# Writing the first gather table from the raw node features instead of the normed ones

## The chip, the core and the metric

The kernel runs on one core of a Trainium2 chip. The core has five engines that run their own instruction streams and wait for each other through counting semaphores: PE (the tensor engine, whose weight loads the profile lists as PEld), DVE (vector), ACT (scalar), POOL (GpSimd) and SP (sync, which only issues transfers here). ACT can issue transfers too, and POOL issues the indirect ones, the gathers. The metric is the device time of one execution in microseconds (us), as the median of several runs.

## The reference, cut to what matters

A graph of 6250 nodes with 256 features and 106250 edges (each drawn edge both ways, and one loop per node, sorted by target) goes through two blocks of graph convolution, linear attention and a mixture of experts. Only the first convolution's beginning matters here:

```python
xn = _layernorm(x, axis=-1)
# L0_gnn: two gcn_conv of xn, each with loops added again
deg  = segment_sum(ones, dst)                 # loops included
dinv = where(deg > 0, rsqrt(deg), 0.0)
h = x @ W
msg = h[src] * (dinv[src] * dinv[dst])[:, None]
out = segment_sum(msg, dst) + b
x + relu(out)
# L0_mix: linear attention over the same xn
```

The kernel gathers rows of `dinv * xn` instead of rows of `h`, sums them by target, multiplies by W afterwards and scales by `dinv` of the target. So before the first gather can start there must be a table in device memory, `t1`, with a row `dinv[n] * xn[n]` for every node n. The normed features `xn` themselves are needed in on-chip memory as well: for the residual and for the attention.

## The kernel before

**Tiles.** Nodes lie in 49 tiles of 128 rows (`NT = 49`, `P = 128`); the tile `xa` (128 x 49 x 256 f32) holds all of them on the chip and is updated in place through the whole kernel. Edges lie in 831 chunks of 128.

**Preparation (lines 332 to 461).** SP loads `dst` and then `x` group by group into `xa`; ACT's queue loads `src` in three pieces (lines 341, 343, 344). DVE casts the indices, PE transposes them, DVE builds one-hots and PE counts the degrees with them (lines 405 to 425), so that `deg` (128 x 49) is there. Beside this, `ln_stats` (line 221) makes mean and variance of each tile on DVE with two instructions, in groups of seven tiles: `rstd` (line 226) takes the square root on ACT and the reciprocal on DVE, line 456 makes `shift = -mean * rs` on DVE, and line 459 norms each tile in place on ACT: `xa = rs * xa + shift`. Then `first_table` (line 314) takes the root of the degrees on ACT, its reciprocal `dinv` on DVE, and writes for every group of four tiles `t1s = dinv * xa`, the even tiles of a group on DVE (line 326) and the odd ones on ACT (line 324), into one of three buffers. SP stores each buffer to `t1` (line 327). Last it makes `rdeg`, which is used much later.

**The branch.** `gflag` says whether the edges are spread so unevenly that a general path is needed. It is worked out from the indices (lines 427 to 449), loaded into a register of every engine (line 463), and every engine branches on it by itself (line 466). With these inputs the general path, which makes the degrees and the table again, is not taken. A second branch on the same register (line 496) is in `general_sums`. At such a branch the framework brings the semaphores of both sides to the same counts: on the skipped side, each engine first waits until its own count (SP: the counts of its transfers) has reached what was issued ahead of the branch, and then adds what the other side would have added. Instructions behind the branch wait for these counts.

**Behind the branch (line 653 on).** SP loads W1 (line 657) and other weights. `neighbour_sums` (line 536) goes through the 831 chunks: POOL gathers the rows of a chunk from `t1` (line 552, four chunks to a buffer, four buffers), DVE makes the one-hots (line 556), PE sums with them (line 575). Between the chunks a planner (`pace`) puts pieces of the attention: PE transposes the normed `xa` (line 259), DVE and ACT copy the two halves out (lines 265 and 263) and PE multiplies them (line 687).

**Order.** From there on PE, SP and POOL keep the order in which the code is written (`ORDERED`); DVE and ACT are ordered by the framework's scheduler. In the preparation the scheduler orders the compute engines; SP's transfers there stand as written.

Of the kernel before, what the change touches and what calls it, by code (L numbers as in the profile page):

```python
# [31 lines left out]
F32 = mybir.dt.float32  # L32
BF16 = mybir.dt.bfloat16
I32 = mybir.dt.int32
AF = mybir.ActivationFunctionType
ALU = mybir.AluOpType
AX = mybir.AxisListType

P = 128
N = 6250  # L40
C = 256
NT = 49
# [21 lines left out]
def groups(size):  # L64
    return [(t0, min(size, NT - t0)) for t0 in range(0, NT, size)]
# [73 lines left out]
def gps_kernel(ctx: ExitStack, tc: tile.TileContext, i: dict, out: bass.AP):  # L139
    nc = tc.nc  # L140
    x_in = i["x"]

    def pool(stack, name, bufs=1, side="left", **kw):
        return stack.enter_context(tc.tile_pool(name=name, bufs=bufs, side=side, **kw))

    consts = pool(ctx, "consts")
    edges = pool(ctx, "edges")
    nodes = pool(ctx, "nodes")
    small = pool(ctx, "small", bufs=3)
# [13 lines left out]
    def ps_mm(name):  # L163
        return ps_tile(name, "mm")
# [9 lines left out]
    def tiles_of(t, t0, n):  # L174

        return t[t0 * P:(t0 + n) * P, :].rearrange("(t p) c -> p t c", p=P)
# [34 lines left out]
    deg = consts.tile([P, NT], F32, name="deg")  # L211
    dinv = consts.tile([P, NT], F32, name="dinv")
    rdeg = consts.tile([P, NT], F32, name="rdeg")
    mv0 = consts.tile([P, NT, 2], F32, name="mv0")
    rs0 = consts.tile([P, NT], F32, name="rs0")
    mv1 = consts.tile([P, NT, 2], F32, name="mv1")
    rs1 = consts.tile([P, NT], F32, name="rs1")
    mv2 = consts.tile([P, NT, 2], F32, name="mv2")
# [2 lines left out]
    def ln_stats(mv, row):  # L221
        st = small.tile([P, 6], F32, name="st", bufs=4)
        nc.vector.bn_stats(st, row)
        nc.vector.bn_aggr(mv, st)

    def rstd(rs, var, n):
        sd = small.tile([P, n], F32, name="sd")
        nc.scalar.activation(sd, var, AF.Sqrt, bias=eps_t, scale=1.0)
        nc.vector.reciprocal(rs, sd)
# [53 lines left out]
    t1 = (dram.tile([NPAD, C], F32, name="t1f"), None)  # L283
# [12 lines left out]
    xa = nodes.tile([P, NT, C], F32, name="xa")  # L296
# [14 lines left out]

    gflag = consts.tile([1, 1], I32, name="gflag")

    def first_table(tp):

        sd = small.tile([P, NT], F32, name="sdeg")
        nc.scalar.activation(sd, deg, AF.Sqrt, bias=ones[:, 0:1], scale=1.0)
        nc.vector.reciprocal(dinv, sd)
        for t0, n in groups(4):
            ts = tp.tile([P, 4, C], F32, name="t1s", bufs=3)  # L320
            for t in range(n):
                T = t0 + t
                if t % 2:
                    nc.scalar.activation(ts[:, t, :], xa[:, T, :], AF.Copy, scale=dinv[:, T:T + 1])
                else:
                    nc.vector.tensor_scalar(ts[:, t, :], xa[:, T, :], dinv[:, T:T + 1], None, op0=ALU.mult)
            nc.sync.dma_start(tiles_of(t1[0], t0, n), ts[:, :n, :])
        dmx = small.tile([P, NT], F32, name="dmax")
        nc.vector.tensor_scalar(dmx, deg, 1.0, None, op0=ALU.max)
        nc.vector.reciprocal(rdeg, dmx)  # L330

    with ExitStack() as st:
        prep = pool(st, "prep")
# [2 lines left out]
        for name, fill, q in (("dst", -1, nc.sync), ("src", 0, nc.scalar)):  # L336
            t = prep.tile([P, NBLK, P], I32, name=f"{name}_pre")
# [44 lines left out]
        for name, to in (("dst", dsti), ("src", sp)):  # L382
            pf = prep.tile([P, NBLK, P], F32, name=f"{name}_pf")
            nc.vector.tensor_copy(pf, pre[name])
            for b0 in range(0, NBLK, 4):
                n = min(4, NBLK - b0)
# [18 lines left out]
        for c0 in range(0, NCH, P):  # L405
            n = min(P, NCH - c0)
# [6 lines left out]
            for c in range(c0, c0 + n):  # L413
# [19 lines left out]
                                op0=ALU.subtract)  # L433
# [14 lines left out]
        nc.vector.tensor_scalar(gpen, gpen, 1.0e6, None, op0=ALU.mult)  # L448
        nc.vector.tensor_scalar(lof, lof, gpen, None, op0=ALU.subtract)

        for t0, n in groups(7):
            for T in range(t0, t0 + n):
                ln_stats(mv0[:, T, :], xa[:, T, :])
            rstd(rs0[:, t0:t0 + n], mv0[:, t0:t0 + n, 1], n)
            shift = small.tile([P, 7], F32, name="shift")
            nc.vector.scalar_tensor_tensor(shift[:, :n], mv0[:, t0:t0 + n, 0], -1.0, rs0[:, t0:t0 + n],
                                           op0=ALU.mult, op1=ALU.mult)
            for T in range(t0, t0 + n):
                nc.scalar.activation(xa[:, T, :], xa[:, T, :], AF.Identity, bias=shift[:, T - t0:T - t0 + 1],
                                     scale=rs0[:, T:T + 1])  # L460
        first_table(pool(st, "table0"))

    general = nc.values_load(gflag[0:1, 0:1], min_val=0, max_val=1,
                             skip_runtime_bounds_check_because="it is the result of a comparison")

    with tc.If(general):
        with ExitStack() as st:
            gw_ = pool(st, "gdeg")
            nc.vector.memset(deg, 0.0)
            hi = gw_.tile([P, NCHP], I32, name="g_hi")  # L470
            nc.vector.tensor_scalar(hi, dsti, 7, None, op0=ALU.arith_shift_right)
            hif = gw_.tile([P, NCHP], F32, name="g_hif")
            nc.vector.tensor_copy(hif, hi)
            nc.vector.tensor_scalar(hi, dsti, P - 1, None, op0=ALU.bitwise_and)
            low = gw_.tile([P, NCHP], F32, name="g_low")
            nc.vector.tensor_copy(low, hi)
            with tc.For_i(0, NCH, 1) as c:
                hc = gw_.tile([P, 1], F32, name="g_hc")
                nc.vector.tensor_copy(hc, hif[:, ds(c, 1)])
                lc = gw_.tile([P, 1], F32, name="g_lc")  # L480
                nc.vector.tensor_copy(lc, low[:, ds(c, 1)])
                oh = gw_.tile([P, NT], F32, name="g_oh")
                nc.vector.tensor_scalar(oh, iota_f[:, :NT], hc, None, op0=ALU.is_equal)
                ol = gw_.tile([P, P], F32, name="g_ol")
                nc.vector.tensor_scalar(ol, iota_f[:, :P], lc, None, op0=ALU.is_equal)
                gd = ps_mm("g_deg")[:, :NT]
                nc.tensor.matmul(gd, lhsT=ol, rhs=oh, start=True, stop=True)
                nc.vector.tensor_add(deg, deg, gd)
        with ExitStack() as st:
            first_table(pool(st, "table1"))  # L490

# [696 lines left out]
    with tc.If(general), ExitStack() as st:  # L1188
# [8 lines left out]
        for j, half in ((OWN[0], 0), (OWN[1], 1)):  # L1197
# [3 lines left out]
                                    op0=ALU.mult, op1=ALU.subtract)  # L1201
# [419 lines left out]
```

## Time and profile before

| what | us |
|---|---|
| median of 7 runs | 4454.25 (4450.22 to 4473.68) |
| the profiled execution | 4441.32 |
| its span, first to last instruction | 4439.3 |
| degree ready (DVE, line 425) | 51.3 |
| in-place norms on ACT (line 459) | 15.8 to 76.2 |
| table tiles on DVE (line 326) | 67.1 to 93.0 |
| table tiles on ACT (line 324) | 71.8 to 91.8 |
| stores of t1, issued by SP (line 327) | 72.8 to 93.0 |
| first gather from t1 (POOL, line 552) | 99.0 |
| last gather from t1 | 1310.3 |

All times are counted from the start of the span. The profiled execution is one run of its own; it lies below the median of the others. How to read the lines that follow: in a timeline a line has the start, the duration (of all of a run of equal instructions, if there is a count), engine, line of the code, operation, result and operands, count, and in brackets the idle time of the engine just before and what ended it; "issue" means that the profile shows nothing that was waited for, "remote" an event whose source it doesn't know. A name with a small q (SPq, ACTq) is the sequencer of an engine, which issues transfers, waits and branches. In a list for one line or tile, the durations are min/median/max in ns, and then come the starts of the first and the last. In a table by stage, each engine has its busy time and, in brackets, its instructions; PEclk is the granted clock of the tensor engine.

### The profile page before, as it was taken

Reading aid. Unit: us, or ns where it says so; the run is one execution under the profiler, and the core shown is the slowest. Engines: PE = TensorE matmul, PEld = TensorE weight load, DVE = VectorE, ACT = ScalarE, POOL = GpSimd, SP = SyncE. Lnnn points to the kernel's source line nnn. Section 1 sums busy time; section 2 is a strip of 40 time slices with the busy share of each in tenths; the row PEclk is TensorE's granted clock in tenths of the full one; section 3 lists DMA queues with packets and bytes.
Section 4 is the critical chain, followed back from the end, with each engine's and each line's share of the span. In section 5 each row is a group of like instructions: output and inputs, shape, how many; then the busy total and the mean of one; then the engine's idle time right before and its main releaser. Section 6 shows DMA issues by size and latency. Waiting matters only on the chain. (4 is left out here: it accounts for less than half of the span.)

```text
span 4439.3 us, 60578 instructions
## 1 busy us (share of the span) xinstructions
PE 3314.5 (75%) x23423; PEld 2722.3 (61%) x23423; DVE 1411.3 (32%) x5300; ACT 981.8 (22%) x2048; POOL 2552.3 (57%) x2665
## 2 busy tenths in 40 slices
PE   3788766766655567777777788883788888888888
PEld 2577656655643445555555665673677777677676
DVE  6222221222121223222232322643343333343333
ACT  3111000000001112222222233441122222222222
POOL 1666666666656666666666555113566666666562
PEclk9888766666676778888888898997799998999998
DMA  4455333333344445555555655575444444444442
GB/s 154 130 169 166 115 113 115 115 113 115 114 122 140 131 129 175 176 178 170 154 166 176 202 180 175 173 255 149 114 133 134 133 132 126 131 132 131 129 130 67
DMA packets 341389, 639.63 MB, mean 144 GB/s; under 512 B 57498, under 2 KB 230341, under 8 KB 341088
## 3 DMA queue, kind: packets, MB, share of 16 engines
q0 software_dynamic: 151872, 450.67, 34.9%
q1 hardware_dynamic: 188366, 184.56, 13.2%
q8 instruction: 185, 3.03, 0.3%
q14 instruction: 116, 0.95, 0.1%
q10 hardware_dynamic: 850, 0.43, 0.0%
HBM read 559.64 MB, written 75.80 MB: 143 GB/s over the span
## 5 line engine op out<-in xcount | busy, mean ns | idle before, releaser
L552 POOL DMA_INDIRECT parts<-t3b,sp x831 | 813.0, 978 | 500.7 <-issue 202.4
L552 POOL DMA_INDIRECT rows<-t1f,sp x831 | 807.2, 971 | 494.2 <-issue 221.7
L552 POOL DMA_INDIRECT parts<-t2b,sp x831 | 805.9, 970 | 468.4 <-issue 220.5
L575 PEld LDWEIGHTS <-parts 128*128 128x128 bf16 x9972 | 604.1, 107 | 377.3 <-issue 167.8
L575 PE MATMUL sums<-onehot,parts 128*128 128x84 bf16 (+2 forms) x9972 | 697.1, 215 | 129.6 <-issue 63.7
L575 PE MATMUL sums<-onehotf,rows 128*128 128x84 f32 (+1 forms) x3324 | 576.2, 325 | 244.8 <-issue 182.4
L575 PEld LDWEIGHTS sums<-onehotf,rows 128*128 128x128 f32 x3324 | 564.1, 244 | 292.2 <-issue 267.9
L902 PE MATMUL hid<-ft,fw 128*128 128x256 f32 (+1 forms) x1824 | 545.0, 438 | 100.0 <-DVE ft L265 35.1
L902 PEld LDWEIGHTS hid<-ft,fw 128*128 128x128 f32 x1824 | 364.2, 217 | 166.2 <-issue 43.6
L556 DVE TENSOR_TENSOR onehot<-iota_w,lof 128x336 bf16<-128x336 bf16 x416 | 210.4, 506 | 752.6 <-PE sums L575 315.6
L904 ACT ACTIVATE ht<-hid,fb 128x256 f32<-128x256 f32 (+1 forms) x456 | 208.7, 472 | 430.3 <-PE hid L902 217.9
L778 PE MATMUL h<-w,aggt 128*128 128x256 f32 x392 | 151.7, 525 | 185.2 <-issue 84.0
L556 DVE TENSOR_TENSOR onehotf<-iota_wf,lof 128x336 f32<-128x336 f32 x208 | 104.7, 507 | 582.2 <-remote 390.8
L1088 PE MATMUL exp<-wd,ht 128*128 128x256 f32 x1024 | 263.2, 395 | 13.4 <-ACT ht L904 6.7
L778 PEld LDWEIGHTS h<-w,aggt 128*128 128x128 f32 x392 | 89.6, 252 | 206.9 <-issue 90.1
L1088 PEld LDWEIGHTS exp<-wd,ht 128*128 128x128 f32 x1024 | 187.1, 193 | 42.1 <-issue 11.1
L595 ACT COPY aggt<-sums 128x88 f32<-128x88 f32 x96 | 22.4, 233 | 828.0 <-PE sums L575 465.4
L1060 POOL DMA_INDIRECT ys<-y,to x64 | 64.0, 1001 | 216.9 <-DVE y L1093 96.0
L1434 PE MATMUL fc_ps<-ht,fc 128*128 128x256 f32 (+1 forms) x600 | 161.6, 392 | 5.8 <-issue 3.1
L1446 PE MATMUL fc_ps<-fc,ut 128*128 128x256 f32 x588 | 160.7, 398 | 6.2 <-issue 6.0
L1434 PEld LDWEIGHTS fc_ps<-ht,fc 128*128 128x128 f32 x600 | 104.7, 192 | 17.9 <-issue 3.7
L1446 PEld LDWEIGHTS fc_ps<-fc,ut 128*128 128x128 f32 x588 | 104.4, 193 | 17.5 <-issue 8.0
(355 smaller groups left out, 4325.3 us busy)
## 6 DMA issues: line engine op xcount, KB each, us to landing
wd<-in_L_ffn_Wd SPq DMA_DIRECT2D x64, 1024.0 KB
xs<-zero SPq DMA_DIRECT2D x8, 1799.0 KB
rows<-t1f,sp POOLq DMA_INDIRECT x831
parts<-t2b,sp POOLq DMA_INDIRECT x831
parts<-t3b,sp POOLq DMA_INDIRECT x831
t2b<-t2s SPq DMA_DIRECT2D x49, 192.0 KB
t3b<-t3s SPq DMA_DIRECT2D x24, 384.0 KB
fs<-xs SPq DMA_DIRECT2D x64, 128.5 KB
```

The source lines that it names most:

```text
L552: nc.gpsimd.indirect_dma_start(out=gs[:, j, :], out_offset=None, in_=(table if f32 else parts)[:, :], in_offset=bass.IndirectOffsetOnAxis( ...
L556: nc.vector.tensor_tensor(ohs[:, :n, :], (iota_wf if f32 else iota_w)[:, None, :WIN].to_broadcast([P, n, WIN]), lof[:, c:c + n, None].to_b ...
L575: nc.tensor.matmul(ps[b][:, h, n0 - b * P:n1 - b * P], lhsT=g[:, k * C + h * P:k * C + (h + 1) * P], rhs=oh[:, n0 - w0:n1 - w0], start=Fal ...
L595: nc.scalar.copy(dst[:, :, WIN:], sums[:, :, WIN:P])
L778: nc.tensor.matmul(h, lhsT=at[:, k, :], rhs=w[:, k, :], start=(k == 0), stop=(k == 1))
L902: nc.tensor.matmul(h_ps[:, :w], lhsT=fw1[:, k, m * P:(m + 1) * P], rhs=ft[:, k, :w], start=(k == 0), stop=(k == 1))
L904: nc.scalar.activation(ht[:, m, :w], h_ps[:, :w], AF.Gelu, bias=fb1[:, m:m + 1], scale=1.0)
L1060: nc.gpsimd.indirect_dma_start(out=ys[v][:, :], out_offset=bass.IndirectOffsetOnAxis(ap=to, axis=0), in_=y, in_offset=None)
L1088: nc.tensor.matmul(y_ps, lhsT=ht[:, m, q * P:(q + 1) * P], rhs=wd[:, m, :], start=(m == 0), stop=(m == 7))
L1434: nc.tensor.matmul(u_ps[:, :w], lhsT=fc1[:, k, m * P:(m + 1) * P], rhs=ht[:, k, :w], start=(k == 0), stop=(k == 1))
L1446: nc.tensor.matmul(h_ps, lhsT=ut[:, m, t * P:(t + 1) * P], rhs=fc2[:, m, :], start=False, stop=(m == 5))
```

## The change

`first_table` is split. Its first and last part, `dinv` and `rdeg`, become `factors`, called as soon as the degrees and the flag are worked out. The table is then made straight from the raw features: for each group of five tiles, DVE makes the statistics, the reciprocal root and `shift` as before, and also `rs * dinv` and `shift * dinv` (the two halves of the new small tile `by`); ACT writes `t1s = (rs * dinv) * xa + shift * dinv` for all five tiles, and SP stores the group. There are three buffers of five tiles. Only when all ten groups are written in the code do the 49 in-place norms on ACT follow, still ahead of the branch. DVE makes no table tile any more. `shift` is kept for all 49 tiles. The general path calls `factors` and the old `first_table` again.

```diff
+    shift = consts.tile([P, NT], F32, name="shift")
...
-    def first_table(tp):
+    def factors():
 
         sd = small.tile([P, NT], F32, name="sdeg")
         nc.scalar.activation(sd, deg, AF.Sqrt, bias=ones[:, 0:1], scale=1.0)
         nc.vector.reciprocal(dinv, sd)
+        dmx = small.tile([P, NT], F32, name="dmax")
+        nc.vector.tensor_scalar(dmx, deg, 1.0, None, op0=ALU.max)
+        nc.vector.reciprocal(rdeg, dmx)
+
+    def first_table(tp):
+
         for t0, n in groups(4):
...
-        dmx = small.tile([P, NT], F32, name="dmax")
-        nc.vector.tensor_scalar(dmx, deg, 1.0, None, op0=ALU.max)
-        nc.vector.reciprocal(rdeg, dmx)
...
-        for t0, n in groups(7):
+        factors()
+        tp = pool(st, "table0")
+        for t0, n in groups(5):
             for T in range(t0, t0 + n):
                 ln_stats(mv0[:, T, :], xa[:, T, :])
-            rstd(rs0[:, t0:t0 + n], mv0[:, t0:t0 + n, 1], n)
-            shift = small.tile([P, 7], F32, name="shift")
-            nc.vector.scalar_tensor_tensor(shift[:, :n], mv0[:, t0:t0 + n, 0], -1.0, rs0[:, t0:t0 + n],
-                                           op0=ALU.mult, op1=ALU.mult)
-            for T in range(t0, t0 + n):
-                nc.scalar.activation(xa[:, T, :], xa[:, T, :], AF.Identity, bias=shift[:, T - t0:T - t0 + 1],
-                                     scale=rs0[:, T:T + 1])
-        first_table(pool(st, "table0"))
+            g = slice(t0, t0 + n)
+            rstd(rs0[:, g], mv0[:, g, 1], n)
+            nc.vector.scalar_tensor_tensor(shift[:, g], mv0[:, g, 0], -1.0, rs0[:, g], op0=ALU.mult, op1=ALU.mult)
+            by = small.tile([P, 2, 5], F32, name="by", bufs=3)
+            nc.vector.tensor_mul(by[:, 0, :n], rs0[:, g], dinv[:, g])
+            nc.vector.tensor_mul(by[:, 1, :n], shift[:, g], dinv[:, g])
+            ts = tp.tile([P, 5, C], F32, name="t1s", bufs=3)
+            for t in range(n):
+                nc.scalar.activation(ts[:, t, :], xa[:, t0 + t, :], AF.Identity, bias=by[:, 1, t:t + 1],
+                                     scale=by[:, 0, t:t + 1])
+            nc.sync.dma_start(tiles_of(t1[0], t0, n), ts[:, :n, :])
+        for T in range(NT):
+            nc.scalar.activation(xa[:, T, :], xa[:, T, :], AF.Identity, bias=shift[:, T:T + 1],
+                                 scale=rs0[:, T:T + 1])
...
+        factors()
         with ExitStack() as st:
             first_table(pool(st, "table1"))
```

## The prediction

> **What bounds the kernel now.** I read the page first, then a table of stages (busy time by stretch), then the timeline of the first 130 us, then single lines of code, and last the lists of what each engine's instructions wait for in the built programs, which hold no times.
>
> ```profile
> PE 3314.5 (75%) x23423; PEld 2722.3 (61%) x23423; DVE 1411.3 (32%) x5300; ACT 981.8 (22%) x2048; POOL 2552.3 (57%) x2665
> ```
> ```profile
> core 0: us, PE busy (x) PEld busy (x) DVE busy (x) ACT busy (x) POOL busy (x), PEclk, DMA share, GB/s
> 0.00:51.30 51.30, 28.28 (x850) 24.99 (x850) 41.78 (x93) 9.73 (x19) 9.27 (x49) 1.00 0.50 156
> 51.30:92.00 40.70, 0.69 (x3) 0.50 (x2) 23.32 (x110) 29.36 (x65) 0.00 (x0) 1.00 0.39 131
> 92.00:99.00 7.00, 0.00 (x0) 0.00 (x0) 1.79 (x4) 0.00 (x0) 0.01 (x1) 1.00 0.61 201
> 99.00:1320.00 1221.00, 852.39 (x4512) 766.11 (x4512) 267.35 (x639) 117.74 (x356) 807.50 (x834) 0.73 0.43 126
> ```
>
> Over the whole span the tensor engine does most. The change touches only 51.3 to 99 us. There the second row shows ACT busy 29.4 of 40.7 us and DVE 23.3, PE and POOL next to nothing: the whole core waits for table t1 to be written, because the first gather reads it at 98.99. So what counts is one moment, the release of the first gather; everything later hangs on it in a row (POOL starts a gather nearly every 1.25 us from there). The chain of waits on the page is traced back only to 3058 us, so I read this moment from the timeline:
>
> ```profile
> 96.77 0.51 DVE L556 TENSOR_TENSOR onehotf<-iota_wf,lof 128x336 f32<-128x336 f32 x1 [3.79 <-SPq L466]
> 96.91 0.39 SPq L657 DMA_DIRECT2D w<-in_L_gnn_W  x1
> 98.99 1.11 POOL L552 DMA_INDIRECT rows<-t1f,sp  x1 [89.07 <-DVE onehotf L556]
> 107.29 0.59 ACT L263 COPY xnt<-xtr 128x512 f32<-128x512 f32 x1 [15.47 <-issue]
> 126.60 0.69 DVE L265 COPY xnt<-xtr 128x512 f32<-128x512 f32 x1 [11.31 <-remote]
> ```
> ```profile
> L466 SPq EVENT_SEMAPHORE  x8: 17/17/17, 95.1 to 96.5; - x8
> L466 ACTq EVENT_SEMAPHORE  x1: 17/17/17, 92.0 to 92.0; - x1
> ```
>
> L466 is the branch around the general path. Its skipped side waits until all that was issued ahead of the branch is done, then passes. SP's eight waits there end at 96.5, when the last store of t1 (issued 93.0) has landed; DVE starts 0.3 us later, SP's load of W1 at 96.91, POOL 2.1 us behind it. ACT was through at 92.0 and then had nothing to do until 107.29.
>
> **The point the rest turns on.** After the branch, the first one-hot on DVE, the W1 load on SP and the first gather on POOL each wait for ACT's count as well. In the changed program that count is 136: 111 of ACT's own, which includes the last of the 49 in-place norms, and 25 from the skipped side, which waits for 111. The norms stand ahead of the branch in the program text, so "behind that" is still ahead of the join. The stores end earlier, but the join moves from SP (96.5) to ACT.
>
> ```profile
> L459 ACT ACTIVATE xa<-xa,shift,rs x49: 583/586/612, 15.8 to 75.6; 128x256 f32<-128x256 f32 x49
> L324 ACT ACTIVATE t1s<-xa,dinv x24: 491/492/510, 71.8 to 91.3; 128x256 f32<-128x256 f32 x24
> L326 DVE TENSOR_SCALAR t1s<-xa,dinv x25: 345/348/354, 67.1 to 92.6; 128x256 f32<-128x256 f32 x25
> ```
> ```profile
> 64.76 6.99 ACT L459 ACTIVATE xa<-xa,shift,rs 128x256 f32<-128x256 f32 x14 [0.30 <-DVE shift L456]
> ```
>
> **The change part by part.** (1) Removed from DVE: 25 scalings of 0.348. They and ACT's 24 waited 20.7 us for stores that moved 340 GB/s; that goes too. Neither is a saving by itself, it depends on ACT below.
> (2) ACT before: 14 of its norms lay ahead of 51.3, in the shadow of the degree count. In the changed order none does: up to the degree ACT has three square roots and two copies. From there it has 49 table tiles and 49 norms, 98 activations. Pitch: 14 of them in 6.99 us, (6.99 - 0.587)/13 = 0.493. The new table tile (bias and scale per row, another tile as output) is not in the trace; nearest below is L324, scale alone, 6 in 2.48 us, pitch 0.41; nearest above is 0.586, the norm's full duration without overlap. I take 0.493, same operands as L459. 98 x 0.493 = 48.3 us (49 x 0.41 lower by 4; all at 0.586 higher by 9).
> (3) Start of these 98. The degree is done at 51.3 (50.74 + 0.55). Then DVE's order up to the first `by`: 0.28 + 0.16 + 0.40 + 0.12 + 0.43 + 0.12 + 0.16 + 0.46 + 0.12 + 0.24 from the rows of these lines = 2.5, less the overlap of some 0.07 each: first table tile about 53.7. The degree itself may come later: ACT's second and third load of `src` (L343, L344, issued at 1.6 and 5.2) now stand behind its first square root, which needs the statistics of tile 4, about 10.3 by DVE's row at 9.46. They are issued near 11, while the loads of x fill the DMA engines at 340 GB/s until about 25 us. DVE casts `src_pre` at 14.56, ahead of all the one-hots of the degree, so a landing past 14.6 shifts all. Between 0 and 2 us; I take 1.
> (4) Seven square roots stay between the activations: two took 0.48, so 1.5. Behind the third and the seventh of them ACT waits for DVE (reciprocal, shift, two products): waits for DVE's shift were 0.30 to 0.69 before, with one norm as filler now; 0.5 each, 1.0.
> (5) Statistics: 32 of 49 remain for DVE after the degree, pitch 0.39, 12.5 us; ACT reaches them later than DVE in both rounds (18 x 0.39 end near 62.6, ACT asks at 62). Nothing on the path; without that cover at most 1.
> (6) Stores: 10 instead of 13 on SP, 640 KB each per 2.5 us of ACT against 1.9 at 340 GB/s, three buffers. Hidden. The last, 512 KB, is issued near 82 and lands about 87: hidden behind the norms (23 us). SP has nothing behind them except the W1 load, which waits for ACT anyway. The extra `by` products (20 on DVE, 0.12 each) and rdeg lie in (3) and (4).
> (7) Behind the join: the instructions of PE, POOL and SP are the same in the same order, DVE's and ACT's too. What is queued: DVE's one-hots, POOL's gathers, SP's W1, W2 and clears, then PE. All norms are then done, as before.
>
> Sum: 51.3 + 1 + 2.4 + 48.3 + 1.5 + 1.0 = 105.5, and 0.2 for the last one's end and the wait (ACT's register load overlapped its last activations before): ACT passes at 105.7 instead of SP at 96.5 with DVE 0.3 later. DVE's one-hot moves from 96.77 to about 105.8, the first gather from 98.99 to 108: **9 us later**. With the bounds: low 9 - 1 - 4 - 1 = +3, high 9 + 1 + 9 = +19.
>
> On the profiled execution (4441.3; its span 4439.3 and 2 around it) that makes 4450. It lay 13 us under the median of the seven runs, 4454.25, so for the median I add the same 9: **4463 us, 0.2% slower**. About 0.3%, 13.4 us, is what a measurement of this kernel tells from no change, so this counts as no change.
>
> A rule speaks against this change: the Trainium skill, page "ScalarE: Activation LUTs", section "Rules for kernel authors", says that multiplying and adding belong on the vector engine rather than the scalar engine. The rows agree for this shape, 0.348 against 0.586. By the rule, half the table tiles stay on DVE (idle between its statistics), ACT saves 25 x 0.493 = 12.3 us, and the change would gain 3 us; as written it loses 9.
>
> **The rivals.**
> *ACT slower than its pitch* (other side). Place: the 98 activations. Price: 0.586 instead of 0.493, 98 x 0.093 = 9.1 us more, +18, 4472. It decides from a mean of 0.54, where the sum passes 13.4. For it: many of them carry a count of their own, and L324, broken up into pairs by waits, takes 0.91 for two. Against it: runs of 7 and 14 keep the pitch. 0.15.
> *One more stall behind the branch* (other side). Between 115 and 127 us DVE, ACT and POOL all stood, with a releaser that the profile doesn't know (11.31 us in the row above). If the new start brings one more such stall, 4463 + 11 = 4474; it decides from 4.5 us. For it: such gaps recur, 1.7% of the span (75 us) in the traced chain. Against it: same instructions behind the join, and DVE, SP and POOL stand ready at the branch some 20 us earlier. 0.17. The Trainium skill, page "Runtime: NRT & Kernel Launch", section "Instruction fetch mechanics", has it that a taken branch out of the fetched window stalls until code is loaded; the trace has one packet of code between 115 and 120 and one between 120 and 126 and names no cause; by that rule the sum stays, since the same branches are taken.
> *The join does not hold* and the gathers start when the stores have landed, near 87 + 2.4. Then the table is 9.5 us earlier, but ACT is still busy with norms until 105.7 and its first copy, 107.29 before, comes at about 106; PE stands in order behind it. Gain between 1.4 and 9.5: 4450. Against it: the counts in the program. 0.08. Even the whole 9.5 stays under 13.4, so faster is hardly open.
>
> **How the numbers follow.** Forecast 0.58, the rivals 0.15, 0.17 and 0.08, others 0.02. Slower: 0.32. Faster: a quarter of the last rival and the others, 0.04. Same: the rest, 0.64. The likeliest case by itself runs from 4457 (+3) to 4467; towards the slower cases I go to 4475, below to 4452 for scatter of the medians.
>
> **What would show it.** In the profile after: last store of t1 issued near 82 and landed near 87; in-place norms on ACT without a break from about 82 to 105.5; first one-hot near 105.8, released by ACT and not by SP; first gather near 108; DVE idle over 30 us ahead of it; from there the same order, ending 9 us later. Wrong: a first gather before 95 (no join on ACT), a pitch of the new table tiles away from 0.49, the degree later than 54, or an end that moved by more than the first gather did.

## The result, and the profile after

| | before | after |
|---|---|---|
| median (runs) | 4459.38 us (63) | 4470.70 us (26) |
| range | 4440.54 to 4481.04 | 4444.36 to 4488.32 |
| ratio after / before | | 1.0024, 95% interval 1.0012 to 1.0035 |
| span of the profiled execution | 4439.3 us | 4457.9 us |

The ratio is 10.7 us (5.4 to 15.6) of 4459.38: a loss too small to count as slower by the 0.3% that the prediction set, though the interval excludes no change.

First the table of stages of the changed kernel (start and end, then busy time and instructions of each engine, the granted clock, the DMA share and GB/s), cut where the degree is done, where the branch opens and where the first gather starts:

```profile
core 0: us, PE busy (x) PEld busy (x) DVE busy (x) ACT busy (x) POOL busy (x), PEclk, DMA share, GB/s
0.00:52.83 52.83, 28.29 (x850) 25.00 (x850) 41.92 (x96) 3.05 (x6) 9.28 (x49) 1.00 0.45 152
52.83:104.80 51.97, 0.71 (x3) 0.50 (x2) 17.85 (x109) 49.91 (x106) 0.00 (x0) 1.00 0.37 125
104.80:107.13 2.33, 0.00 (x0) 0.00 (x0) 1.44 (x3) 0.00 (x0) 0.00 (x0) 1.00 0.45 117
```

In the second row ACT is busy 49.9 of 52.0 us, DVE 17.9, and everything else has next to nothing to do. In the kernel before, ACT had done part of its work in the shadow of the degree count; of that, 9.73 us ahead of the degree have become 3.05 here. The timeline shows what ACT does, and who starts when it stops (start, length, engine, line, operation, count, and in brackets the idle time before it with what ended it):

```profile
55.15 7.48 ACT L470 ACTIVATE t1s<-xa,by 128x256 f32<-128x256 f32 x15 [1.95 <-DVE by L467]
...
57.74 24.30 SPq L472 DMA_DIRECT2D t1f<-t1s  x10
62.53 0.67 ACT L229 ACTIVATE sd<-mv,eps_t 128x5 f32<-128x5 f32 x3
63.10 0.59 ACT L474 ACTIVATE xa<-xa,shift,rs 128x256 f32<-128x256 f32 x1
...
72.22 9.43 ACT L470 ACTIVATE t1s<-xa,by 128x256 f32<-128x256 f32 x19
...
81.55 23.17 ACT L474 ACTIVATE xa<-xa,shift,rs 128x256 f32<-128x256 f32 x47
104.79 0.38 SPq L672 DMA_DIRECT2D w<-in_L_gnn_W  x1
104.80 0.51 DVE L571 TENSOR_TENSOR onehotf<-iota_wf,lof 128x336 f32<-128x336 f32 x1 [29.76 <-ACTq L480]
...
107.13 1.11 POOL L567 DMA_INDIRECT rows<-t1f,sp  x1 [97.20 <-DMA w<-in_L_gnn_W]
```

The waits at the branch (L480) of the same kernel:

```profile
L480 SPq EVENT_SEMAPHORE  x8: 17/17/17, 83.2 to 85.0; - x8
...
L480 DVEq EVENT_SEMAPHORE  x1: 21/21/21, 75.7 to 75.7; - x1
...
L480 ACTq EVENT_SEMAPHORE  x1: 17/17/17, 104.8 to 104.8; - x1
```

The table is complete at 81.6 and has landed at 85.0, 11.5 us earlier than before (96.5). The one-hot on DVE still stands until 104.80, 29.76 us, and its releaser is ACT's wait at the branch: the 47 norms from 81.55 to 104.72 are all that the core does for 20 us. The first gather starts 8.1 us later than before (107.13 against 98.99). The bracket at the gather names the load of W1, which itself was let go at 104.79 by the branch.

The single profiled spans differ by 18.6 us, more than that. The gathers show where: 8.1 us at the first gather, 6.6 at the last one from the first table, 7.7 and 11.9 at the two ends of the second table, 16.3 and 21.8 at those of the third. They are two executions out of ranges 40 us wide; a second pair, below, differs by 11.1.

### The profile page after: what moved, and what is told of

Its sections match the earlier page's. It is cut to its first block, busy times and chain, and to the rows that moved or that the text cites. A ratio compares the mean times of both kernels' runs of the same rounds, so it can differ in the third digit from the quotient of the medians.

```text
span 4457.9 us, 60590 instructions
## 1 busy us (share of the span) xinstructions
PE 3329.0 (75%) x23423; PEld 2736.8 (61%) x23423; DVE 1407.6 (32%) x5301; ACT 997.1 (22%) x2076; POOL 2554.5 (57%) x2665
## 2 busy tenths in 40 slices
DMA packets 341341, 639.63 MB, mean 143 GB/s; under 512 B 57450, under 2 KB 230293, under 8 KB 341040
## 5 line engine op out<-in xcount | busy, mean ns | idle before, releaser
L590 PE MATMUL sums<-onehotf,rows 128*128 128x84 f32 (+1 forms) x3324 | 593.0, 332 | 275.9 <-issue 210.1
L590 PEld LDWEIGHTS sums<-onehotf,rows 128*128 128x128 f32 x3324 | 582.0, 251 | 319.4 <-issue 295.9
L917 PE MATMUL hid<-ft,fw 128*128 128x256 f32 (+1 forms) x1824 | 534.7, 432 | 90.7 <-DVE ft L266 34.3
L1103 PEld LDWEIGHTS exp<-wd,ht 128*128 128x128 f32 x1024 | 189.2, 196 | 44.3 <-issue 11.7
L1425 PE MATMUL att<-wf,xnt 128*128 128x256 f32 x196 | 74.2, 528 | 64.6 <-DVE xnt L266 41.9
L1449 PEld LDWEIGHTS fc_ps<-ht,fc 128*128 128x128 f32 x600 | 105.4, 194 | 16.9 <-issue 5.2
```

What stands on the lines that cost most here:

```text
L590: nc.tensor.matmul(ps[b][:, h, n0 - b * P:n1 - b * P], lhsT=g[:, k * C + h * P:k * C + (h + 1) * P], rhs=oh[:, n0 - w0:n1 - w0], start=Fal ...
L917: nc.tensor.matmul(h_ps[:, :w], lhsT=fw1[:, k, m * P:(m + 1) * P], rhs=ft[:, k, :w], start=(k == 0), stop=(k == 1))
L1103: nc.tensor.matmul(y_ps, lhsT=ht[:, m, q * P:(q + 1) * P], rhs=wd[:, m, :], start=(m == 0), stop=(m == 7))
L1425: nc.tensor.matmul(ps, lhsT=xnt[:, k, t * P:(t + 1) * P], rhs=wf[:, k, :], start=(k == 0), stop=(k == 1))
L1449: nc.tensor.matmul(u_ps[:, :w], lhsT=fc1[:, k, m * P:(m + 1) * P], rhs=ht[:, k, :w], start=(k == 0), stop=(k == 1))
```

## The experiments

The runs were made on three chips. The kernel before took 3903.44 us on the chip of the first four, 4455.78 on that of the next four and 3914.08 on that of the last four. Ratios are to the kernel before on the same chip. The changed kernel as it stands was run on the second of these chips and for the result above, where the kernel before takes 4456 to 4459 us; on the two faster chips it was not, so a ratio from there shows what a variant gains on the kernel before, and not on the changed one.

### Does the branch wait for ACT?

The kernel before, with work for ACT added ahead of the branch:

```diff
         first_table(pool(st, "table0"))
+        idle = prep.tile([P, C], F32, name="idle")
+        for _ in range(30):
+            nc.scalar.activation(idle, xa[:, NT - 1, :], AF.Copy, scale=dinv[:, 0:1])
```

> The kernel before, with 30 useless ACT scalings of one tile (128x256) added behind the last table tile, ahead of the branch; nothing of the result changes. Theory (the branch waits for whichever engine ends last, and all of that reaches the end): ACT, done at 92.0 in the kernel before, ends at 92.0 + 30 x 0.493 = 106.8; the first one-hot on DVE moves from 96.77 to 106.8, the first gather from 98.99 to 109.0, the time by +10 us (ratio about 1.0022). Rival (the branch waits for the stores alone, and the loss of the changed kernel comes from its later degree or from further down): the first gather stays at 99.0 and the time is the same.

Measured: 1.0003 (0.9991 to 1.0015). ACT passed the branch at 99.5, not at 106.8, since 16 of the 30 had slipped into the gaps between its table tiles; the first gather came at 101.64. The releaser was ACT as the theory has it, but the dose was too small to be seen in the time. With 60:

> The kernel before with 60 instead of 30 useless ACT scalings ahead of the branch. With 30, 16 filled ACT's gaps and only 14 stood behind the last table tile, so the dose was small. Here 44 stand behind it. Theory (what ACT adds ahead of the branch reaches the end in full): ACT ends at 92 + 44 x 0.493 = 114, first one-hot at 114, first gather at 116.3, 17 us later than in the kernel before; time +17 us, ratio 1.0038 on a chip on which before takes 4456, 1.0044 where it takes 3903. Rival (a later stage takes some of it up): first gather at 116, but the ratio under 1.002.

Measured: 1.0051 (1.0037 to 1.0065), 20 us (14 to 25). The waits at the branch and DVE's first one-hot:

```profile
L469 SPq EVENT_SEMAPHORE  x8: 17/17/17, 95.2 to 96.6; - x8
...
L469 ACTq EVENT_SEMAPHORE  x1: 17/17/17, 116.6 to 116.6; - x1
```
```profile
116.60 0.51 DVE L559 TENSOR_TENSOR onehotf<-iota_wf,lof 128x336 f32<-128x336 f32 x1 [23.61 <-ACTq L469]
```

The stores had landed at 96.6, where the kernel before goes on; the branch opened with ACT at 116.6, 20 us later, and the time grew by 20 us. What ACT adds ahead of this branch reaches the end, in full as far as the interval tells. (The 44 last scalings had a pitch of 0.54, not 0.493, hence 116.6 instead of 114. They have the form of L324, whose pitch was 0.41, but all write one and the same tile; whether that is the reason was not tried.)

### The kernel before and the changed kernel on one chip

> The kernel before, unchanged, profiled on the chip that the experiments run on: the four runs so far took some 3900 us where the recorded ones took 4460, so the yardsticks at the branch have to be read on the same chip. Theory (what lies ahead of the branch is no faster here; the difference between the chips arises behind it): first one-hot at 96 to 97, first gather at 98 to 99, as recorded. Rival (everything is faster here by the 12%): degree at 45, first gather at 87.

Measured: 4451.43, one run; first one-hot at 97.28, first gather at 99.51. This chip turned out to be of the recorded kind, so the question of the faster one was answered elsewhere: on the chip of 3903 us the kernel with 30 added scalings had its stores landed at 96.0 and its first gather at 101.64. Ahead of the branch the chips are alike.

> The changed kernel, unchanged, beside the kernel before on this chip. Theory (the branch opens with ACT's last norm, 49 + 49 operations of 0.493 us behind a degree at 52.4): first one-hot at 104.3, first gather at 106.6, 8 us behind the kernel before, and these 8 us reach the end: ratio 1.0020 with this kernel's time (3903). Rival (part of the recorded loss arises further down): the first gather 8 us late, but the ratio 1.003 or more; or the delay is taken up by a stage further down that waits for something else: ratio 1.000.

Measured: 1.0020 (0.9999 to 1.0040). The gathers of the three tables, in the kernel before and then in the changed one (count, duration, first and last start):

```profile
L552 POOL DMA_INDIRECT rows<-t1f,sp x831: 940/946/1943, 99.5 to 1312.0; - x167
L552 POOL DMA_INDIRECT parts<-t2b,sp x831: 940/946/1261, 1328.4 to 2769.1; - x167
L552 POOL DMA_INDIRECT parts<-t3b,sp x831: 940/946/1944, 3070.8 to 4388.9; - x167
```
```profile
L567 POOL DMA_INDIRECT rows<-t1f,sp x831: 943/949/1276, 107.3 to 1320.4; - x167
L567 POOL DMA_INDIRECT parts<-t2b,sp x831: 942/949/1343, 1336.6 to 2781.0; - x167
L567 POOL DMA_INDIRECT parts<-t3b,sp x831: 942/949/1938, 3083.0 to 4401.9; - x167
```

The difference is 7.8 us at the first gather, 8.4 at the end of that stage, 8.2 at the start of the next, 12 to 13 from its end on, and 11.1 at the end. The first 8 us stay. In both pairs a few us more come behind the second table; they are of the size by which single executions differ, and two pairs cannot tell more.

### Taking the norms out of the branch's way

The 49 norms written behind the branch, in one block. The general path, which reads the nodes too, makes its table from the raw rows with product columns instead:

```diff
             nc.sync.dma_start(tiles_of(t1[0], t0, n), ts[:, :n, :])
-        for T in range(NT):
-            nc.scalar.activation(xa[:, T, :], xa[:, T, :], AF.Identity, bias=shift[:, T:T + 1],
-                                 scale=rs0[:, T:T + 1])
...
             first_table(pool(st, "table1"))
+    for T in range(NT):
+        nc.scalar.activation(xa[:, T, :], xa[:, T, :], AF.Identity, bias=shift[:, T:T + 1],
+                             scale=rs0[:, T:T + 1])
```

> The changed kernel with its 49 in-place norms written behind the branch instead of ahead of it (all on ACT; the general path makes its table from the raw rows with the product columns). Theory: ACT is through with the table at 81.6, the stores have landed at 85.0; the branch opens there: first one-hot at 85.3, first gather at 87.6, 19.5 us less than in the changed kernel and 11.4 less than before. ACT's norms then run from 85 to 108.5, and the first ACT copy of the transposed nodes, which would come at 96, waits behind them until 108.5: up to 12.4 us of the 11.4 may be given back there if PE needs that buffer, nothing if it does not. Ratio to before 0.9974 to 1.0002. Rival (the loss of the changed kernel does not come from the norms ahead of the branch): ratio stays 1.002 although the norms are gone from there.

Measured: 0.9970 (0.9959 to 0.9981), 11.7 us less than before. The timeline:

```profile
81.25 24.19 ACT L510 ACTIVATE xa<-xa,shift,rs 128x256 f32<-128x256 f32 x49
...
84.71 0.51 DVE L577 TENSOR_TENSOR onehotf<-iota_wf,lof 128x336 f32<-128x336 f32 x1 [10.18 <-SPq L483]
...
87.28 1.11 POOL L573 DMA_INDIRECT rows<-t1f,sp  x1 [77.36 <-ACT xa L510]
```

The same norms run at the same time as in the changed kernel, but the releaser of the one-hot is SP's wait for the stores again, and the gathers no longer wait for the norms: the first starts 18 us ahead of the last norm's end at 105.4. (The bracket at the gather names one of these norms; in the repeat of this kernel below it names the load of W1.) This is the part of the change that decides: the same table and the same stores, and 11.7 us less than before instead of 10.7 more, though the two were measured on chips of different speed.

The norms then hold ACT until 105.4, and its first copy of the transposed nodes comes behind them. Whether that costs anything was asked with the norms of four tiles placed just ahead of these tiles' transposes:

```diff
         for gi, (t0, n) in enumerate(gs):
+            for T in range(t0, t0 + n):
+                nc.scalar.activation(xa[:, T, :], xa[:, T, :], AF.Identity, bias=shift[:, T:T + 1],
+                                     scale=rs0[:, T:T + 1])
             transposed(xnt[:, :, t0 * P:(t0 + n) * P], lambda t: xa[:, t0 + t, :], n, "xtr", vs)
```

> The changed kernel with the norms of each group of four tiles written just ahead of that group's transposes, behind the branch, instead of all 49 in one block there. Theory (the branch opens with the stores at 84.7 to 85, as with the block; ACT's first copies of the transposed nodes no longer stand behind 24 us of norms): first gather at 87.3, first ACT copy of the transposed nodes at 95 to 97 instead of 105; if that copy was on the path, up to 9 us less than with the block, ratio 0.9948 to 0.997. Rival (the copy is hidden by PE's sums, which wait for gathers): the same time as with the block, ratio 0.997.

Measured: 0.9992 (0.9977 to 1.0006), first gather at 88.16. That is 11.4 us earlier than in the kernel before on the same chip, and a time that fell by 3.6 us (10.2 less to 2.7 more). This is also the one chip of the three that had the changed kernel: with the norms at their use its first gather comes 19.1 us earlier (88.16 against 107.3) and its median is 17.1 us lower (4448.43 of 12 runs against 4465.49 of 9). The two placements were then run side by side.

> The kernel with the 49 norms in one block behind the branch once more, beside the one with the norms at their use, so that both are read on one chip. Theory (ACT's first copy of the transposed nodes, 9 to 10 us late behind the block, is covered by PE's sums): branch and first gather as in the other (85 to 86, 87.3 to 88.2), the same ratio within 0.1%. Rival (the late copy holds PE): this one 3 to 9 us slower than the one with the norms at their use.

> The kernel with the norms at their use once more, beside the block. Its first measurement was 0.9992 with an interval that reaches 1.0006, while the block, on another chip, had 0.9970. Theory: both gain what the branch gains, 11.4 us: ratio 0.9974 where before takes 4456, 0.9971 where it takes 3903. Rival (norms between the copies, 17 of ACT's first 20 operations behind the branch, hold up the copies of the nodes and of the sums): 0.999 again, over 4 us slower than the block.

Measured: block 0.9966 (0.9952 to 0.9980), at their use 0.9972 (0.9962 to 0.9982). ACT's first copy of the transposed nodes, block first, then at their use:

```profile
106.15 0.56 ACT L264 COPY xnt<-xtr 128x512 f32<-128x512 f32 x1
```
```profile
95.92 0.58 ACT L264 COPY xnt<-xtr 128x512 f32<-128x512 f32 x1 [9.35 <-PE xtr L260]
```

The copy is 10.2 us later and the time the same: the last gather of the first table starts at 1157.9 and 1157.1. The medians are 3901.35 and 3905.10, so the give-back that the first expectation allowed for is not seen. That the placement at the use had only 0.9992 on the other chip did not repeat here; whether the gain is smaller on chips of that kind stays open, and the block was not run there.

### Sharing ACT's work with DVE

Every second tile of a group made on DVE:

```diff
+                if t % 2:
+                    nc.vector.tensor_scalar(ts[:, t, :], xa[:, t0 + t, :], by[:, 0, t:t + 1], by[:, 1, t:t + 1],
+                                            op0=ALU.mult, op1=ALU.add)
+                else:
                     nc.scalar.activation(ts[:, t, :], xa[:, t0 + t, :], AF.Identity, bias=by[:, 1, t:t + 1],
                                          scale=by[:, 0, t:t + 1])
```

> The changed kernel with every second table tile made on DVE (multiply and add with the same two columns), the norms left on ACT. Theory: ACT loses 20 of its 49 table tiles (two of each group of five), 20 x 0.493 = 9.9 us, so it ends at 104.7 - 9.9 = 94.9; DVE's 20 tiles at 0.31 to 0.35 us (6 to 7 us) fit in, since DVE was through at 75.7. First one-hot at 95, first gather at 97.2: 10 us less than in the changed kernel and 1.8 us less than before; ratio to before 0.9996. Rival (ACT's pace is set by DVE's statistics and by columns, not by its own work): ACT ends at 104 as before and the time stays 1.002.

Measured: 1.0003 (0.9992 to 1.0013), first gather at 96.71. The waits at the branch:

```profile
L484 SPq EVENT_SEMAPHORE  x8: 17/17/17, 80.2 to 82.3; - x8
...
L484 DVEq EVENT_SEMAPHORE  x1: 21/21/21, 77.2 to 77.2; - x1
L484 ACTq EVENT_SEMAPHORE  x1: 17/17/17, 94.3 to 94.3; - x1
```

ACT ends 10.5 us earlier than in the changed kernel and is still the last by 12 us. With that the loss is no longer seen, and no gain either; a gain of the 2 us by which the first gather is earlier than the 98.99 before could not be told.

With the in-place norms alternately on DVE and ACT as well (the same `if` around them):

> As the one with the divided table, and every second in-place norm on DVE as well. Theory: ACT ends 24 x 0.493 = 11.8 us earlier again, at 83.1; DVE, through at 75.7 in the changed kernel, takes 44 more operations of 0.31 to 0.35 us and ends at 89 to 91; the branch opens with DVE then, at 89 to 91, the first gather at 91 to 93.5: 6 to 8 us less than before, ratio 0.9982 to 0.9987. Rival (the stores set the branch once the norms are shared): it opens when the stores have landed, 85 or a little later, gather at 87.5, ratio 0.9974. Second rival (what the branch gains is lost again further down): first gather early, ratio 1.000 or more.

Measured: 0.9980 (0.9971 to 0.9989), 7.8 us less than before, first gather at 86.63. The three engines now reach the branch almost together:

```profile
L488 SPq EVENT_SEMAPHORE  x8: 17/17/17, 80.4 to 82.3; - x8
...
L488 ACTq EVENT_SEMAPHORE  x1: 17/17/17, 82.7 to 82.7; - x1
L488 DVEq EVENT_SEMAPHORE  x1: 21/21/21, 84.2 to 84.2; - x1
```

DVE came last, as expected, but at 84.2 and not at 89 to 91: its 19 last norms took 6.22 us, and the tiles before them went in part where DVE had waited for ACT in the changed kernel, 3.9 us there and none here. The gather started 0.65 us earlier than with the norms behind the branch on the same chip. The median is 4.6 us longer, but the two intervals overlap, so no difference is shown.

Table divided and norms at their use:

> The kernel with the norms at their use and every second table tile on DVE. Theory (with the norms gone the branch opens when the stores have landed, and these are limited by the transfer: ten stores of some 650 KB took 27.3 us both where the last one was issued at 82 and where it was issued at 78): the branch opens at 84 to 85, first gather at 86.2 to 87, 1 us before the kernels with the whole table on ACT; ratio within 0.0005 of theirs. Rival (stores wait for table tiles): the last tile is done 4 to 9 us earlier and the first gather comes at 79 to 84.

Measured: 0.9969 (0.9959 to 0.9979), first gather at 86.18. SP's wait for the stores ends at 83.5 instead of 84.8, with the issue of the last store ended at 80.2 instead of 81.8. So the stores end 3.0 to 3.4 us behind the issue of the last one and still follow the last table tile, as the rival has it and not the theory; but that tile is done only 1.6 us earlier, not 4 to 9, and 1.3 us is all that this brings. In the time it cannot be told.

### Why was the degree late?

> The changed kernel with the three loads of src issued on SP, behind those of dst, instead of on ACT, where the second and third stood behind the first square root. Theory (the degree came 1.5 us later because DVE's cast of src waited for those loads): that wait of 2.2 us is gone, the degree is back at 51 to 51.5, and ACT, which works without a gap from there to the branch, ends 1 to 1.5 us earlier: first gather at 105.2 to 105.8. Rival (the degree is held by the matmuls on the one-hots, not by src): degree and first gather unchanged, 52.5 and 106.8.

Measured: one run, 4448.94, not to be told from the others. DVE in the changed kernel on this chip, and then in this one:

```profile
16.64 0.63 DVE L388 CAST src_pf<-src_pre 128x896 f32<-128x896 int32 x1 [2.14 <-DMA src_pre<-in_src]
...
22.92 2.29 DVE L412 TENSOR_TENSOR ob<-bb,iota_b 128x2048 bf16<-128x2048 bf16 x1
25.12 1.09 DVE L415 TENSOR_TENSOR oa<-ab,iota_b 128x896 bf16<-128x896 bf16 x1
...
48.53 0.55 DVE L423 COPY d<-deg 16x392 f32<-16x392 f32 x1 [1.48 <-PE deg L419]
...
52.26 0.55 DVE L429 TENSOR_REDUCE deg<-dm 128x49 f32<-128x392 f32 x1
```
```profile
14.94 0.60 DVE L388 CAST src_pf<-src_pre 128x896 f32<-128x896 int32 x1
...
20.54 2.29 DVE L412 TENSOR_TENSOR ob<-bb,iota_b 128x2048 bf16<-128x2048 bf16 x1
22.74 1.02 DVE L406 TENSOR_TENSOR ab<-ai,alo 128x831 bf16<-128x831 int32 x1
23.67 2.29 DVE L412 TENSOR_TENSOR ob<-bb,iota_b 128x2048 bf16<-128x2048 bf16 x1
25.88 2.09 DVE L415 TENSOR_TENSOR oa<-ab,iota_b 128x896 bf16<-128x896 bf16 x2
...
49.30 0.55 DVE L423 COPY d<-deg 16x392 f32<-16x392 f32 x1 [1.78 <-PE deg L419]
...
52.30 0.54 DVE L429 TENSOR_REDUCE deg<-dm 128x49 f32<-128x392 f32 x1
```

The wait of 2.14 us for src is gone, so it did come from the late loads. But the last step of the degree starts at 52.30 instead of 52.26. PE's matmuls for the degree need a pair of one-hots, `ob` and `oa`, and from the first whole pair to DVE's copy of their result it is 22.3 us in both kernels (26.2 to 48.5, and 27.0 to 49.3). The scheduler ordered DVE anew and put the second `ob` ahead of the first `oa`, so the first pair is whole no earlier, although its work began 2.4 us earlier. The expected 1.5 us did not come, the first gather stayed at 107.11. So this run does not show what the degree would gain if src alone came earlier.

## Why the prediction was right, point by point

The forecast was 9 us at the first gather and as much at the end; measured were 8.1 (7.8 in the second pair) and 10.7 (5.4 to 15.6).

- *The point it turned on*, that the norms stand ahead of the join and the join moves from SP to ACT: shown. The releaser is ACT's wait at L480; norms behind the branch give 0.9970 and 0.9966; 20 us more of ACT in the kernel before cost 20 us.
- *(2), 98 activations at 0.493*: right. Fifteen table tiles in 7.48 us are (7.48 - 0.587)/14 = 0.492, the 47 norms (23.17 - 0.586)/46 = 0.491. The bounds 0.41 and 0.586 were not needed.
- *(3), start*: the degree came at 52.83, 1.5 us later, where 1 was taken of 0 to 2. DVE's cast of src waited 2.23 us for the load, as argued, and started 1.8 us later than before; that this wait alone made the degree late is not shown. The way from the degree to the first table tile was 2.32 (2.4 predicted), but that agreement is luck: the ten terms listed make 2.5, which ten overlaps of 0.07 bring down to 1.8, and what was measured holds two waits of DVE for PE, 0.16 and 0.29 us, that the list leaves out.
- *(4), square roots and handshakes*: too high. From 55.15 to 104.72 are 49.57 us; less 98 x 0.493 leaves 1.3 for both, where 2.5 were counted. The waits for DVE were covered: a norm and the roots of the next round filled them.
- *(5)*: right; ACT waited for no statistics. *(6)*: landed at 85.0 (87 predicted), hidden by the norms. *(7)*: the order behind the branch was the same; ACT's first copy of the transposed nodes came 8.0 us later, as the gather did.
- *Sum*: ACT passed at 104.8 against 105.7. The errors of (3) and (4) had opposite signs, so that the sum came within 1 us is in part luck.
- *The absolute time*: 4463 against 4470.7. The base was 5 us low: the median of seven runs was 4454.25, that of 63 is 4459.38. The rest is 10.7 or 11.3 against 9, within the interval.
- *The rule weighed* (the Trainium skill, "ScalarE: Activation LUTs", "Rules for kernel authors"): right in its direction. The two rows set beside each other are not of the same operation, though: for scaling alone it is 0.348 on DVE against 0.492 on ACT (L324). With 20 table tiles on DVE no loss was left (1.0003), on a chip of the faster kind. The gain of 3 us that was worked out for it cannot be told from nothing.
- *The sign of being wrong that comes near*: the end moved by 10.7, more than the first gather with 8.1. The interval (5.4 to 15.6) holds both, and the 60 scalings moved both alike (the first gather stood at 118.67, 19.7 us behind the recorded one, and the end 20 us behind), so nothing further down is shown to have its part.
- *The rivals*: the pitch of 0.586 fell with the rows. No further stall came: the one behind the branch is there in both (DVE's second copy of the transposed nodes waited 11.31 before and 10.61 after, for "remote"). The join that does not hold fell with the releaser; but the gain named for its case, at most 9.5, is near what moving the norms brings (11.7 and 13.3 on the faster chips; 3.6, with 10.2 at most, on the chip of the recorded kind), and the part of it that feared ACT's late copy was wrong where it was tried: the copy is hidden.

No version found is clear of the simplest one: the changed kernel with the norms in a block behind the branch takes 0.9970 (0.9959 to 0.9981) and 0.9966 (0.9952 to 0.9980) of the kernel before, both on chips of the faster kind.

## To carry to other kernels

A branch, even one that is never taken, can be a join of all engines: what is written ahead of it is waited for, whether or not the work behind it needs it. Look for the releaser at the branch and put work that is needed later behind it. When a change frees one engine and loads another, add up the loaded engine to the next join first; and a dose of useless work on that engine ahead of the join tells in one run whether its time reaches the end, if the dose is larger than the gaps that it fills.

## What was not expected of the hardware

The same kernel takes 4459 and 4456 us in two series and 3903 and 3914 in two others on other chips, 12% less, though granted clocks differ by 4% (0.833 against 0.863 in profiled runs of the kernel before and of it with 30 more scalings). DMA bytes and packets are alike (639.63 MB). PE was busy for 3314.5 us as recorded and for 3216.0 us in the run with 30 more scalings, from a chip of the faster kind; of the 534 us by which these two spans differ, 436 are idle time of PE. In the list of waits (engine, tile, line, what it waited for: us in total, times, longest) the kernel before has, as recorded:

```profile
DVE onehotf L556 <- remote: 390.8, 61, 13.7
...
PEld sums L575 <- issue: 267.9, 276, 51.7
PE sums L575 <- issue: 246.0, 333, 2.3
```

and the run with 30 more scalings:

```profile
DVE onehotf L559 <- PE sums L578: 524.5, 173, 11.2
...
PEld sums L578 <- issue: 93.3, 84, 55.2
```

There "remote" (a releaser that the profile does not know) ends none of the listed waits, and PE's matmuls have 0.2 us of "issue" in all, against 246.0 for their sums alone. The one-hots themselves do not wait much less there. Those of the first table (`onehotf`) have 390.8 for "remote" and 116.0 for PE's sums as recorded, and 524.5 for PE's sums in the other run; those of the later tables (`onehot`) 217.0 and 315.6, and 469.1. What is longer on the slower kind of chip is above all time in which PE stands and the profile shows nothing that it waits for.

Ahead of the branch the two kinds of chip agree to 1 us. What holds PE there was not tried, and the changed kernel itself was not run on a chip of the faster kind.
